# A graph layer on one core: node-block register loads merged, two carries a unit apart, gate values in PSUM, 32 column groups on VectorE

## The chip, the core and the metric

The kernel runs on one core of a Trainium2 chip. The core has five engines with queues of their own: TensorE (PE; its weight loads are PEld), VectorE (DVE), ScalarE (ACT), GpSimd (POOL) and SyncE (SP). The last two, and ScalarE, can start DMAs. An engine works through its queue in order; between engines semaphores wait and signal. The metric is the device time of one execution in microseconds, as the median of several runs.

## The reference

A message-passing layer over 12500 nodes with 128 features and 400000 edges, sorted by target node, followed by a GRU cell:

```python
h = relu(layernorm(x))                                     # 12500 x 128
m = relu(concat(h[src], h[dst], ea) @ w1 + b1) @ w2 + b2   # 400000 x 128, ea 400000 x 32
agg = segment_sum(m, dst, 12500)
gi, gh = agg @ w_ih + b_ih, h @ w_hh + b_hh                # split in r, z, n
r, z = sigmoid(gi_r + gh_r), sigmoid(gi_z + gh_z)
n = tanh(gi_n + r * gh_n)
out = x + (1 - z) * n + z * h
```

## The kernel before

**Layout.** A first stage normalizes all nodes, keeps h transposed in SBUF (`hT_all`, features on partitions, one column a node) and writes two products to DRAM, A = h @ w1[0:128] for the sources and B = h @ w1[128:256] + b1 for the targets. Then come the edges: 391 groups of 1024 edges, each handled as two *units* of 512, so 782 units. The Python loop over u writes every engine's instructions unit by unit; the order in which each engine works is fixed by it (the schedule is manual).

**A group.** TensorE forms the target's and the edge attributes' part of the message in `pre` (L763). The source's part comes in one of four ways, dealt out before the loop by the table `SPREAD`:

- GpSimd *gathers* rows of A by indirect DMA, 128 rows at a time, 8 gathers a group (L193). VectorE adds them to `pre` (L792, a saturating add that is also the relu). The first 9 groups gather rows of x.
- ScalarE *brings* a group's 1024 columns of `hT_all`, one 4-byte copy for each (L1103) into `HE_act`; the addresses come from register loads of 16. TensorE multiplies them by w1[0:128] into `pre` (L774), VectorE does the relu (L786). 29 groups.
- VectorE does the same for 31 groups, two columns an instruction (L1061), and reorders 256 columns at a time (L1073). Its register loads take up to 32 values (L1050).
- SyncE fetches single rows of A for 5 groups.

TensorE then sums the messages into windows of 32 nodes (L814).

**What sets the order.** ScalarE's and SyncE's groups are spread evenly over the units up to their use (`run_jobs`); VectorE's follow a table of what is due by each unit, and are fitted in small lots between its other work (`some`, `behind_long`, `in_time`). GpSimd's gathers are released by a credit, four times a unit, each tied behind the latest column instruction or VectorE instruction at that point (`let_go`). The register that a unit's steps set, `worked`, decides how many columns VectorE does behind the unit.

**The node blocks.** Every 14 groups a block of nodes is complete: 29 blocks, 26 of them 512 nodes wide. `node(b)` is a generator; one piece of it is written at the end of a unit, and `yield n` puts the next piece n units later. Its steps: the windows' sums are placed (L842, L847); what reaches over from the block before is added, in `carry` for the sums (`TOT`) and for the degrees (`DEG`) (L853, L856); the gates r, h_n, i_n and z follow (L892, L894, L896), in two PSUM banks by turns, "nd" and "misc"; ScalarE does the sigmoid of r (L902), tanh (L914) and the sigmoid of z (L916); VectorE the products and sums between (L906, L910, L920, L923, L926); TensorE transposes, VectorE adds x (L933), SyncE writes the output. Where a block begins is data, so its first node is a register value: `blk_i` holds the first nodes and `step_i` how far each block lies from the one before; VectorE (L861, L918), TensorE (L885) and SyncE (L830) each load theirs with `value_load`, which checks the value on the engine after the load. `last_node` is the same for the last block, in steps near the end of the loop.

Of the kernel before, what the change touches and what calls it, by code (L numbers as in the profile page):

```python
# [11 lines left out]
I32 = mybir.dt.int32  # L12
# [3 lines left out]
ET = mybir.EngineType  # L16
AF = mybir.ActivationFunctionType
ALU = mybir.AluOpType
# [36 lines left out]
STEP = {"act": 4, "sp": 4}  # L55
QUEUE = 10
ROW = 4 * D
SPREAD = {"dve": 31, "act": 29, "sp": 5}
START = {"dve": 14, "act": -6, "sp": 28}
SPARE = ("HE_act", "HE_dve", "G_sp")  # L60
NR = 12672
# [6 lines left out]
def tile_gnn(ctx: ExitStack, tc: tile.TileContext, x, src, srcT, dstT, dstP, eaT, eaP, w1, b1, w2T, b2,  # L68
# [253 lines left out]

    base_f = const.tile([1, NP], F32, name="base_f")
    blk_f = const.tile([1, NB], F32, name="blk_f")
    blk_i = const.tile([1, NB], I32, name="blk_i")
    off_f = const.tile([1, NB, 16], F32, name="off_f")
    off_i = const.tile([1, NB, 16], I32, name="off_i")
    base_i = const.tile([1, NB, 16], I32, name="base_i")
    step_f = const.tile([1, NB], F32, name="step_f")
    step_i = const.tile([1, NB], I32, name="step_i")  # L330
    step_c = const.tile([1, NB], F32, name="step_c")
    dloc = const.tile([128, T], F16, name="dloc")
    lim = const.tile([128, 2, NPL], F32, name="lim")
# [26 lines left out]
    def setup(pool):  # L360
        nc.vector.tensor_copy(base_f[:, 1:], base_d)
        nc.vector.memset(base_f[:, 0:1], 0.0)
        nc.vector.tensor_scalar(base_f, base_f, float(LAST), 0.0, op0=ALU.min, op1=ALU.max)
        yield
        nc.vector.tensor_copy(at_f[64:65, 512:512 + NP], base_f)
        nc.vector.tensor_tensor(at_f[64:65, :NP], at_f[64:65, 512:512 + NP], at_f[64:65, :NP], op=ALU.is_gt)
        nc.vector.tensor_reduce(beyond, at_f[64:65, :NP], AX.X, ALU.max)
        yield
        pm = ps1.tile([128, 512], F32, name="misc")
        nc.tensor.matmul(pm[:, :NP], ones, base_f, start=True, stop=True)  # L370
        nc.vector.tensor_copy(base_b[:, :, 0], pm[:, :NP])
        yield
        nc.vector.tensor_scalar(base_b[:, :, 1], pm[:, :NP], float(SHIFT), None, op0=ALU.add)
        for a in range(2):
            s = slice(V * a, V * (a + 1))
            nc.vector.tensor_scalar(node_of[s, :], base_b[s, :, a], place_c[s, :], float(-V * a),
                                    op0=ALU.add, op1=ALU.add)
        for b0, b1_, k0, n, w in groups:
            nc.vector.tensor_scalar(blk_f[:, b0:b1_], base_f[:, k0:k0 + (b1_ - b0 - 1) * n + 1:n], float(N - w),
                                    None, op0=ALU.min)  # L380
        yield
        nc.vector.tensor_copy(blk_i, blk_f)
        nc.vector.memset(off_f, 0.0)
        off_c = pool.tile([128, NB * 16], F32, name="off_c", bufs=1)[:1, :].rearrange("o (b n) -> o b n", n=16)
        yield
        nc.vector.memset(off_c, 0.0)
        nc.vector.tensor_tensor(step_f[:, 1:], blk_f[:, 1:], blk_f[:, :-1], op=ALU.subtract)
        nc.vector.memset(step_f[:, 0:1], float(BW))
        yield
        for b0, b1_, k0, n, w in groups:  # L390
            ks = base_f[:, k0:k0 + (b1_ - b0) * n].rearrange("o (b n) -> o b n", n=n)
            nc.vector.tensor_tensor(off_f[:, b0:b1_, :n], ks,
                                    blk_f[:, b0:b1_, None].to_broadcast([1, b1_ - b0, n]), op=ALU.subtract)
            nc.vector.tensor_scalar(base_i[:, b0:b1_, :n], ks, float(4 * D), None, op0=ALU.mult)
            nc.vector.tensor_scalar(off_c[:, b0:b1_, :n], off_f[:, b0:b1_, :n], float(w - V - SHIFT), 0.0,
                                    op0=ALU.min, op1=ALU.max)
        for b0, b1_ in [(0, 1), (1, NW + 1)] + [(b, b + 1) for b in range(NW + 1, NB)]:
            nc.vector.tensor_scalar(step_c[:, b0:b1_], step_f[:, b0:b1_], float(BLOCKS[max(b0 - 1, 0)][2]),
                                    float(LEAST[b0]), op0=ALU.min, op1=ALU.max)
        nc.vector.tensor_copy(off_i, off_c)  # L400
        yield
        nc.vector.tensor_tensor(off_f, off_f, off_c, op=ALU.not_equal)
        nc.vector.tensor_copy(step_i, step_c)
        nc.vector.tensor_tensor(step_f, step_f, step_c, op=ALU.not_equal)
        yield
        yield
        place(0)
# [417 lines left out]
        worked[0] = 1  # L825


    def block_start(b):
        k0, n, w = BLOCKS[b]
        g0 = nc.sync.value_load(blk_i[0:1, b:b + 1], min_val=0, max_val=N - w)  # L830
        xb = p3.tile([128, 4, D], F32, name="xb", bufs=2)[:w // 4, :, :]
        put(xb, x[bass.ds(g0, w), :].rearrange("(p i) f -> p i f", i=4))
        _, offs = nc.values_load_multi_w_load_instructions(
            off_i[0:1, b, 0:n], engines=[ET.PE], min_val=0, max_val=w - V - SHIFT,
            skip_runtime_bounds_check_because="clamped above")
        return g0, xb, offs
# [21 lines left out]
            nc.vector.memset(o[:, w:last], 0.0)  # L858

    def step_of(b):  # L860
        return nc.vector.value_load(step_i[0:1, b:b + 1], min_val=LEAST[b],  # L861
                                    max_val=BLOCKS[max(b - 1, 0)][2])

    def temp(w):
        return p3.tile([128, BW], F32, name="gt", bufs=3)[:, :w]
# [1 line left out]
    def node(b):  # L867
        w = BLOCKS[b][2]
        g0, xb, offs = block_start(b)
        pt = ps1.tile([128, 512], F32, name="nd")[:, :w]  # L870
        pd = ps1.tile([128, 512], F32, name="misc")[:, :w]
        nc.vector.tensor_copy(dcol[:, :len(offs) // 2], sums[:, :len(offs) // 2, D])
        zero(pt)
        for i in range(len(offs)):
            sum_of(b, pt, offs, i)
        zero(pd)
        for i in range(len(offs)):
            degree_of(b, pd, offs, i)
        d = step_of(b)
        yield 1  # L880
        carry(b, TOT, pt, d)
        carry(b, DEG[0:1, :], pd[0:1, :], d)
        worked[0] = 2
        yield 1
        g = nc.tensor.value_load(blk_i[0:1, b:b + 1], min_val=0, max_val=N - w)  # L885
        hT = hT_all[:, bass.ds(g, w)]

        def gate(name, i, with_h, with_s):
            c = slice(i * D, (i + 1) * D)
            ci = slice(2 * D, 3 * D) if i == 3 else c  # L890
            pg = ps1.tile([128, 512], F32, name=name)[:, :w]
            nc.tensor.matmul(pg, brow[:, c], DEG[:, :w], start=True, stop=False)  # L892
# [9 lines left out]
        nc.scalar.activation(r, pr, AF.Sigmoid)  # L902
        ph = gate("misc", 3, True, False)
        yield 1
        t = temp(w)
        nc.vector.tensor_tensor(t, r, ph, op=ALU.mult)  # L906
        pi = gate("nd", 2, False, True)
        worked[0] = 2
        yield 1
        nc.vector.tensor_tensor(t, t, pi, op=ALU.add)  # L910
        pz = gate("misc", 1, True, True)
        worked[0] = 2
        yield 2 if b < NW else 1
        nc.scalar.activation(t, t, AF.Tanh)  # L914
        z = temp(w)
        nc.scalar.activation(z, pz, AF.Sigmoid)  # L916
        yield 1
        gv = nc.vector.value_load(blk_i[0:1, b:b + 1], min_val=0, max_val=N - w)  # L918
# [7 lines left out]
        nc.vector.tensor_tensor(q, q, t, op=ALU.add)  # L926
# [12 lines left out]
        batch_store(b + FIRST)  # L939

    def last_node():
# [5 lines left out]
        zero(pd)  # L947
        for i in range(n):
            degree_of(b, pd, offs, i)
        d = step_of(b)  # L950
        g = nc.tensor.value_load(blk_i[0:1, b:b + 1], min_val=0, max_val=N - w)
        hT = hT_all[:, bass.ds(g, w)]
        gv = nc.vector.value_load(blk_i[0:1, b:b + 1], min_val=0, max_val=N - w)
        h = hT_all[:, bass.ds(gv, w)]
        pt = ps1.tile([128, 512], F32, name="nd")[:, :w]
        zero(pt)
# [500 lines left out]
```

## Time and profile before

| | |
|---|---|
| runs | 4668.68, 4675.16, 4681.94 us (median 4675.16) |
| the profiled execution | 4666.41 us, its span 4664.6 us |
| ScalarE busy | 3272.2 us (70%), 29939 instructions |
| VectorE busy | 2548.3 us (55%), 18124 instructions |
| TensorE busy | 2538.9 us (54%), 13193 matmuls |
| GpSimd busy | 2485.7 us (53%), 2614 instructions |
| DMA | 71 GB/s over the span |

A row of the groups reads: line, engine, operation, what it writes and reads, the shape, how often | busy microseconds, mean nanoseconds of one | idle microseconds of the engine just before, and what ended that idle time. A copy of four bytes is reported with 189 ns, but the next one starts before it has ended: busy time counts overlapping instructions once. A row of the waits reads: engine, tile and line that waited, who released it, microseconds in total, times, the longest. A row of the windows reads: from and to, length, then for PE, PEld, DVE, ACT and POOL the busy microseconds and the number of instructions, then TensorE's granted clock, the DMA share and GB/s. Operations marked "q" (register loads, checks) are the sequencer's and not counted as busy.

### The profile page before, as it was taken

How to read it: one execution, taken by the hardware profiler on the slowest of the kernel's cores; microseconds unless marked ns; L12 is line 12 of the kernel's file. 1: busy time of each engine (PE TensorE's matmuls, PEld its weight loads, DVE VectorE, ACT ScalarE, POOL GpSimd, SP SyncE). 2: the span in 40 equal slices, each digit the busy share in tenths (PEclk: the TensorE clock that was granted, in tenths of full speed). 3: DMA queues.
4: the chain of work that ended last, by engine and by line, in shares of the span. 5: the costliest groups of instructions: out<-in, count | busy, mean ns of one | idle time of the engine just before them, and what ended most of it. 6: DMA issues, size and time to landing. Idle time of an engine off the chain costs nothing. (4 is left out here: it accounts for less than half of the span.)

```text
span 4664.6 us, 96852 instructions
## 1 busy us (share of the span) xinstructions
PE 2538.9 (54%) x13193; PEld 1611.8 (35%) x13193; DVE 2548.3 (55%) x18124; ACT 3272.2 (70%) x29939; POOL 2485.7 (53%) x2614
## 2 busy tenths in 40 slices
PE   2465565565456455555555565455545454655657
PEld 2353342332234233323333333333323233323434
DVE  3475564564456446645654565456546555655655
ACT  2478667767767767777777767777776777676676
POOL 5345555555555555555555555555555555555551
PEclk7786767776667767776776667677767767767767
DMA  3322323222222223232222223232322322222221
GB/s 103 105 65 60 75 71 74 69 71 70 69 72 73 71 71 73 66 78 69 72 70 68 73 71 79 60 73 69 74 69 72 81 63 72 68 73 69 72 73 35
DMA packets 195490, 333.37 MB, mean 71 GB/s; under 512 B 68809, under 2 KB 117512, under 8 KB 194841
## 3 DMA queue, kind: packets, MB, share of 16 engines
q0 software_dynamic: 83360, 170.89, 16.0%
q1 hardware_dynamic: 111337, 156.20, 12.2%
q14 instruction: 539, 4.42, 0.3%
q8 instruction: 110, 1.80, 0.2%
q10 hardware_dynamic: 144, 0.07, 0.0%
HBM read 306.65 MB, written 20.24 MB: 70 GB/s over the span
## 5 line engine op out<-in xcount | busy, mean ns | idle before, releaser
L1103 ACT COPY HE_act<-hT_all 128x4 uint8 x29696 | 3169.2, 189 | 1255.9 <-issue 1223.5
L193 POOL DMA_INDIRECT G<-A,src_i x2512 | 2396.4, 954 | 2052.2 <-ACT HE_act L1103 1329.8
L1061 DVE SCALAR_TENSOR_TENSOR both<-hT_all 128x4 uint16 x15872 | 1365.4, 154 | 649.4 <-issue 635.6
L763 PE MATMUL pre<-RW,L 128*128 128x256 f32 x3128 | 1163.5, 499 | 536.3 <-DVE L L650 295.9
L763 PEld LDWEIGHTS pre<-RW,L 128*128 128x128 f32 x3128 | 681.9, 243 | 842.2 <-issue 433.3
L814 PE MATMUL seg<-RB,OH 128*32 128x129 f32 x6250 | 607.9, 325 | 270.2 <-DVE RB L792 158.4
L814 PEld LDWEIGHTS seg<-RB,OH 128*32 128x32 f32 x6250 | 334.4, 125 | 573.1 <-issue 308.9
L892 PE MATMUL nd<-DEG,brow 34*128 34x512 f32 (+2 forms) x112 | 89.0, 886 | 761.3 <-ACT gt L902 614.2
L792 DVE CUSTOM_DVE_ANT_0 RB<-pre,G 128x1024 f32<-128x1024 f32 x315 | 383.2, 1217 | 117.5 <-issue 62.9
L906 DVE TENSOR_TENSOR gt<-gt,misc 128x512 f32<-128x512 f32 (+2 forms) x28 | 18.9, 675 | 677.8 <-ACT gt L902 545.9
L892 PEld LDWEIGHTS nd<-DEG,brow 34*128 34x128 f32 x112 | 22.4, 248 | 775.7 <-ACT gt L902 620.8
L650 DVE TENSOR_TENSOR L<-L,seg 64x1024 f32<-64x1024 int32 x191 | 230.5, 1207 | 40.4 <-issue 16.4
L774 PE MATMUL pre<-w1a,HE_act 128*128 128x128 f32 x464 | 96.0, 328 | 255.0 <-ACT HE_act L1103 230.7
L786 DVE TENSOR_SCALAR RB<-pre 128x1024 f32<-128x1024 f32 x69 | 84.2, 1221 | 213.1 <-PE pre L774 154.4
L774 PEld LDWEIGHTS pre<-w1a,HE_act 128*128 128x128 f32 x464 | 90.0, 235 | 271.2 <-ACT HE_act L1103 235.6
L703 DVE TENSOR_TENSOR OH<-dloc,seg 128x512 f32<-128x512 f16 (+1 forms) x198 | 132.9, 672 | 17.6 <-issue 17.6
L842 PE MATMUL nd<-spot,sums 128*128 128x40 f32 x782 | 139.0, 358 | 2.8 <-DVE sums L823 2.8
L842 PEld LDWEIGHTS nd<-spot,sums 128*128 128x128 f32 x782 | 134.6, 270 | 13.7 <-issue 10.6
L1073 DVE COPY HE_dve<-both 128x1024 uint8<-128x1024 uint8 x124 | 88.6, 715 | 24.8 <-issue 15.7
L774 PEld LDWEIGHTS pre<-w1a,HE_dve 128*128 128x128 f32 x496 | 90.3, 226 | 14.1 <-remote 2.0
L920 DVE TENSOR_TENSOR gt<-hT_all,gt 128x512 f32<-128x512 f32 (+2 forms) x28 | 19.1, 680 | 134.3 <-ACT gt L914 109.3
L774 PE MATMUL pre<-w1a,HE_dve 128*128 128x128 f32 x496 | 89.3, 309 | 3.0 <-remote 1.7
(185 smaller groups left out, 1473.5 us busy)
## 6 DMA issues: line engine op xcount, KB each, us to landing
G_sp<-A SPq DMA_DIRECT2D x5120, 0.5 KB
L<-in_dstP SPq DMA_DIRECT2D x195, 256.0 KB
L<-in_eaP SPq DMA_DIRECT2D x195, 256.0 KB
G<-A,src_i POOLq DMA_INDIRECT x2512
RW<-B SPq DMA_DIRECT2D x782, 16.0 KB
xb<-in_x SPq DMA_DIRECT2D x26, 256.0 KB
out<-xb SPq DMA_DIRECT2D x26, 256.0 KB
xs<-in_x SPq DMA_DIRECT2D x11, 512.0 KB
```

The source lines that it names most:

```text
L193: fetched = nc.gpsimd.indirect_dma_start(out=G[k][:, j, a, :], out_offset=None, in_=x if k < RAW else A, in_offset=bass.IndirectOffsetOnAx ...
L650: recent[0] = nc.vector.tensor_tensor(o.rearrange("v (k e) -> v k e", k=m), i.rearrange("v (k e) -> v k e", k=m), SEGB[(k // 2) % 2][:2 * ...
L703: recent[0] = nc.vector.tensor_tensor(p, dloc[:, e0:e1, None].to_broadcast(shape), row[:, None, :].to_broadcast(shape), op=ALU.is_equal).ins
L763: nc.tensor.matmul(p[:, 2 * i:2 * i + 2, :], Ls[k // QP][:, c0:c0 + 128], RW[k % 4], start=True, stop=not raw)
L774: nc.tensor.matmul(p[:, 2 * i + a, :], cols, w1a, start=False, stop=n + 1 == len(l) or l[n + 1][1] != j)
L792: made = nc.vector._custom_dve(TENSOR_ADD_SAT, out=o, in0=p, in1=G[k].rearrange("p j a f -> p (j a) f")[:, c, :], s0=float("inf"), s1=0.0)
L814: nc.tensor.matmul(p[r0:r0 + V, :D + 1], OH[k][:, a * GRP + j, :], RB[k % 2][:, 2 * j + a, :D + 1], start=False, stop=all(b != a for _, _, ...
L842: nc.tensor.matmul(p[:, bass.ds(offs[i], V + SHIFT)], sums[:, slot(b, i), :D], spot[:, i % 2, :], start=False, stop=i == len(offs) - 1)
L892: nc.tensor.matmul(pg, brow[:, c], DEG[:, :w], start=True, stop=False)
L1061: recent[0] = nc.vector.scalar_tensor_tensor(self.both[:, e % PIECE // 2, :], column(second), 256.0, column(first), op0=ALU.mult, op1=ALU. ...
L1073: recent[0] = nc.vector.tensor_copy(hand[k].bitcast(U8)[:, p0 * 4:(p0 + PIECE) * 4].rearrange("p (n c b) -> p n c b", c=2, b=4), both.bitc ...
L1103: copied[0] = nc.scalar.copy(he[:, e * 4:e * 4 + 4], column(v)).ins
```

## The change

Four edits. VectorE's share in `SPREAD` goes from 31 groups to 32, so GpSimd gathers for one group less; the places of the other hand-brought groups shift by a group or so. In the node blocks the distance and the first node stand side by side in `off_i`; VectorE loads both in one load at the start of the block, and all engines load without the check on the engine. The two carries are written a unit apart in 26 blocks, which puts all later steps of these blocks a unit later. The value that goes into tanh and its result stay in the PSUM bank "nd" instead of an SBUF tile, and the z gate stays in "misc".

```diff
-SPREAD = {"dve": 31, "act": 29, "sp": 5}
+SPREAD = {"dve": 32, "act": 29, "sp": 5}
...
-        nc.vector.tensor_copy(step_i, step_c)
+        nc.vector.tensor_copy(off_i[:, :, 14], step_c)
+        nc.vector.tensor_copy(off_i[:, :, 15], blk_f)
...
+    def first_of(engine, b):
+        _, (g,) = nc.values_load_multi_w_load_instructions(
+            off_i[0:1, b, 15:16], engines=[engine], min_val=0, max_val=N - BLOCKS[b][2],
+            skip_runtime_bounds_check_because="clamped above")
+        return g
...
     def block_start(b):
         k0, n, w = BLOCKS[b]
-        g0 = nc.sync.value_load(blk_i[0:1, b:b + 1], min_val=0, max_val=N - w)
+        g0 = first_of(ET.SP, b)
...
     def step_of(b):
-        return nc.vector.value_load(step_i[0:1, b:b + 1], min_val=LEAST[b],
-                                    max_val=BLOCKS[max(b - 1, 0)][2])
+        _, (d, g) = nc.values_load_multi_w_load_instructions(
+            off_i[0:1, b, 14:16], engines=[ET.DVE], min_val=0, max_val=N - BLOCKS[b][2],
+            skip_runtime_bounds_check_because="clamped above")
+        return nc.s_assert_within(d, LEAST[b], BLOCKS[max(b - 1, 0)][2],
+                                  skip_runtime_bounds_check_because="clamped above"), g
...
-        d = step_of(b)
+        d, gv = step_of(b)
         yield 1
         carry(b, TOT, pt, d)
+        worked[0] = 2
+        if b < NW:
+            yield 1
         carry(b, DEG[0:1, :], pd[0:1, :], d)
         worked[0] = 2
         yield 1
-        g = nc.tensor.value_load(blk_i[0:1, b:b + 1], min_val=0, max_val=N - w)
+        g = first_of(ET.PE, b)
...
-        t = temp(w)
-        nc.vector.tensor_tensor(t, r, ph, op=ALU.mult)
-        pi = gate("nd", 2, False, True)
+        nc.vector.tensor_tensor(r, r, ph, op=ALU.mult)
+        t = gate("nd", 2, False, True)
         worked[0] = 2
         yield 1
-        nc.vector.tensor_tensor(t, t, pi, op=ALU.add)
+        nc.vector.tensor_tensor(t, r, t, op=ALU.add)
         pz = gate("misc", 1, True, True)
...
         nc.scalar.activation(t, t, AF.Tanh)
-        z = temp(w)
-        nc.scalar.activation(z, pz, AF.Sigmoid)
+        z = pz
+        nc.scalar.activation(z, z, AF.Sigmoid)
         yield 1
-        gv = nc.vector.value_load(blk_i[0:1, b:b + 1], min_val=0, max_val=N - w)
         q = r
```

In `last_node` the same loads are replaced: `step_of` and `first_of` in place of three `value_load`.

VectorE's queue at the two carries of a block in the middle of the program, before (`TOT` and `DEG` are the carried sums and degrees, `both` and `at` belong to the columns):

```order
L1061 SCALAR_TENSOR_TENSOR both<-hT_all 128x4 x3
L853 ISA
L853 TENSOR_TENSOR TOT<-nd,TOT 128x192
L856 COPY TOT<-nd 128x320
L853 ISA
L853 TENSOR_TENSOR DEG<-misc,DEG 1x192
L856 COPY DEG<-misc 1x320
```

and in the changed kernel, whose line numbers differ by a few (L790 is the addition of a gathered group):

```order
L857 TENSOR_TENSOR TOT<-nd,TOT 128x192
L860 COPY TOT<-nd 128x320
L1068 SCALAR_TENSOR_TENSOR both<-hT_all 128x4 x9
L1057 TENSOR_LOAD at
L1068 SCALAR_TENSOR_TENSOR both<-hT_all 128x4 x3
L790 ISA RB_179<-pre,G 128x8x128
L1068 SCALAR_TENSOR_TENSOR both<-hT_all 128x4 x9
L1057 TENSOR_LOAD at
L1068 SCALAR_TENSOR_TENSOR both<-hT_all 128x4 x7
L857 ISA
L857 TENSOR_TENSOR DEG<-misc,DEG 1x192
L860 COPY DEG<-misc 1x320
```

Two lots of columns with their register loads and a group's addition now stand between the carries.

VectorE's queue in the last block, before, from the last pair of windows' sums to the carry of the degrees:

```order
L861 TENSOR_LOAD step_i
L861 ISA x2
L953 TENSOR_LOAD blk_i
L953 ISA x2
L792 ISA RB_180<-pre,G 128x8x128
```

and in the changed kernel:

```order
L821 COPY sums<-seg_80 128x129
L865 TENSOR_LOAD off_i
L790 ISA RB_180<-pre,G 128x8x128
L857 ISA
L857 TENSOR_TENSOR DEG<-misc,DEG 1x192
```

One load without checks has taken the place of two loads with two checking steps each, ahead of a group's addition.

More of the change, by code (lines that the diff above doesn't have):

```diff
@@ L324, in tile_gnn @@
     blk_f = const.tile([1, NB], F32, name="blk_f")
-    blk_i = const.tile([1, NB], I32, name="blk_i")
     off_f = const.tile([1, NB, 16], F32, name="off_f")
@@ L381, in setup @@
         yield
-        nc.vector.tensor_copy(blk_i, blk_f)
         nc.vector.memset(off_f, 0.0)
@@ L949, in last_node @@
             degree_of(b, pd, offs, i)
-        d = step_of(b)
-        g = nc.tensor.value_load(blk_i[0:1, b:b + 1], min_val=0, max_val=N - w)
+        d, gv = step_of(b)
+        g = first_of(ET.PE, b)
         hT = hT_all[:, bass.ds(g, w)]
-        gv = nc.vector.value_load(blk_i[0:1, b:b + 1], min_val=0, max_val=N - w)
         h = hT_all[:, bass.ds(gv, w)]
```

1 line of the change is left out of this document (removed).

## The prediction

> **What bounds the kernel now.** I read the page's costliest groups first, to see which engine never rests, then the waits, to see who waits for whom.
>
> ```profile
> L1103 ACT COPY HE_act<-hT_all 128x4 uint8 x29696 | 3169.2, 189 | 1255.9 <-issue 1223.5
> L193 POOL DMA_INDIRECT G<-A,src_i x2512 | 2396.4, 954 | 2052.2 <-ACT HE_act L1103 1329.8
> L1061 DVE SCALAR_TENSOR_TENSOR both<-hT_all 128x4 uint16 x15872 | 1365.4, 154 | 649.4 <-issue 635.6
> L193 POOL DMA_INDIRECT G<-in_x,src_i x69 | 65.2, 945 | 21.9 <-issue 20.7 <-DMA src_i<-in_srcT 1.2
> ```
> ```profile
> POOL G L193 <- ACT HE_act L1103: 1329.8, 660, 16.0
> DVE gt L906 <- ACT gt L902: 545.9, 22, 36.2
> PE nd L892 <- ACT gt L902: 614.2, 22, 40.7
> ```
>
> Everyone waits for ScalarE. GpSimd holds its gathers for ScalarE's column copies (1329.8 us), and once in each node block VectorE and TensorE stand still until ScalarE has reached the sigmoid of r (545.9/22 = 24.8 us each time for VectorE). ScalarE itself waits for no engine between its first and its last copy: its idle time before the copies is 1255.9 us, of which 1223.5 are "issue", time in which it waited for nothing that the profile shows. Its timeline gives the two ends:
>
> ```profile
> 168.15 2.90 ACT L1103 COPY HE_act<-hT_all 128x4 uint8 x27 [1.07 <-DVE bn L255]
> ...
> 4629.23 3.58 ACT L1103 COPY HE_act<-hT_all 128x4 uint8 x36
> 4654.88 0.44 ACT L991 ACTIVATE gt<-pre 128x320 f32<-128x320 f32 x1 [22.07 <-PE pre L972]
> ```
>
> So the time is a head of 168.2 us, ScalarE's stretch of 4464.7 us up to 4632.8, and a tail of 31.8 us. The chain of waits on the page follows only the last microseconds and says nothing about this. An edit counts if it changes ScalarE's copies, its activations, its "issue" time, the head or the tail. What is that "issue" time? Four stretches of the windows view tell (per engine: busy us and instructions):
>
> ```profile
> 172.00:222.00 50.00, 5.73 (x24) 5.07 (x24) 9.86 (x45) 7.94 (x41) 37.81 (x41) 0.56 0.32 85
> 4430.00:4445.00 15.00, 0.00 (x0) 0.00 (x0) 0.00 (x0) 11.62 (x110) 8.38 (x10) 0.50 0.33 79
> 4574.00:4616.00 42.00, 32.00 (x171) 19.70 (x171) 30.66 (x210) 41.01 (x415) 0.00 (x0) 0.72 0.16 48
> ```
> ```profile
> 1271.12:1439.27 168.15, 94.76 (x500) 60.69 (x499) 95.65 (x689) 112.23 (x1028) 93.59 (x97) 0.72 0.30 73
> 1439.27:1577.33 138.06, 76.93 (x405) 47.50 (x405) 76.04 (x573) 107.72 (x1027) 76.25 (x81) 0.72 0.29 71
> ```
>
> From 4574 on there are no gathers: ScalarE does 415 instructions in 42.00 us (0.101 us each), busy for 41.01, although VectorE and TensorE work at full rate. From 4430 on they are silent and GpSimd sends 10 gathers in 15 us: ScalarE manages 110, worth 11.1 us, and loses 3.9. From 172 on 41 gathers follow each other closely and ScalarE does 41 instructions in 50 us. So gathers stop ScalarE. The last two rows are two of its groups, each of 1024 copies; the first is spread over 30 units of the program, the second over 24. The first takes 30.1 us longer for the same copies, and what it has more of is 16 gathers, 116 VectorE instructions and 95 matmuls. **The bound is ScalarE's copies plus what gathers, perhaps together with VectorE's and TensorE's work, take from them.**
>
> **The change part by part.**
>
> *The 32nd group.* It leaves GpSimd's list: 8 gathers fewer. What one takes from ScalarE is at least 3.9/10 = 0.39 us (the quiet stretch) and at most 30.1/16 = 1.88 us (all of the difference between the two groups). I take the middle, 1.1: 8 x 1.1 = **-8.8 us** (-3.1 to -15.0).
>
> VectorE gets 512 two-column instructions, four reorderings and 35 register loads more. On VectorE itself that is 512 x (1365.4 + 649.4)/15872 = 65 us, 2.3 us in each of 28 blocks, and the wait of 24.8 us hides it; with that cover gone it would be 65 us. What it takes from ScalarE no row isolates. Below, the stretch without gathers says nothing. Above, if all 1223.5 us of "issue" belonged to the 15872 column instructions, 0.077 us each. Two windows with nearly the same gathers give the same upper end:
>
> ```profile
> 1200.00:1600.00 400.00, 204.49 (x1063) 126.90 (x1063) 205.81 (x1511) 292.60 (x2721) 225.48 (x235) 0.71 0.28 69
> 2400.00:2800.00 400.00, 234.45 (x1161) 144.78 (x1159) 229.94 (x1685) 279.42 (x2587) 221.75 (x234) 0.68 0.29 71
> ```
>
> In the second ScalarE does 134 fewer (13.6 us) beside 174 more on VectorE and 98 more on TensorE: 0.078 if VectorE alone were to blame, 0 if TensorE were. I take 0.02, nearer to the stretch without gathers, the only row where the columns' effect stands alone: 512 x 0.02 = **+10.2 us** (0 to +39.4). That the register loads hold up VectorE is in the 649.4.
>
> Here the Trainium skill speaks against the change. Its page Perfetto Trace Analysis, section Optimizing Scalar/DVE Operations, says that GpSimd and VectorE share a read port of SBUF, so that moving work between those two might not help. The trace shows no such lengthening: a gather's instruction takes 954 ns beside the columns and 945 ns before there are any (the rows of L193). By that difference all 2512 would have lost 23 us in an engine that idles for 2052.
>
> *Register loads in one, unchecked.* The lines' own view gives what goes on VectorE and TensorE:
>
> ```profile
> L861 DVEq TENSOR_LOAD <-step_i x29: 304/307/619, 387.6 to 4638.2; - x29
> L861 DVEq FUSED_REGOPS  x29: 183/190/210, 388.0 to 4638.9; - x29
> L861 DVEq SEQ_ASSERT  x29: 23/23/41, 388.3 to 4639.1; - x29
> L918 DVEq TENSOR_LOAD <-blk_i x28: 304/308/535, 451.5 to 4627.2; - x28
> ```
> ```profile
> L885 PEldq TENSOR_LOAD <-blk_i x28: 300/306/320, 393.9 to 4605.4; - x28
> L885 PEldq FUSED_REGOPS  x28: 151/151/165, 394.3 to 4605.9; - x28
> ```
>
> VectorE saves 0.19 + 0.02 of checks, twice, and one load of 0.31: 0.73 us a block, 20 us in all; TensorE saves 0.17 a block. Both lie under the wait for the sigmoid and cost the end nothing; SyncE's same load only fetches the rows of x that the block adds in its last step. Some 260 small sequencer steps go from VectorE, TensorE and SyncE together. If such a step weighs on ScalarE like a column, that is -5.2, and 0 by the stretch without gathers; I take **-2.5 us**.
>
> *Carries a unit apart.* Nothing is added: the same four instructions, with columns and a group's addition between them. All later steps of 26 blocks come one unit (4464.7/782 = 5.7 us) later, ScalarE's three activations too. TensorE's gate r now waits for the later carry, behind whose wait VectorE holds columns and a group's addition; both reach it a good 20 us ahead of ScalarE, by the 24.8 us above, so this costs 0; if that lead were gone, up to 5.7 us a block.
>
> *Gates in PSUM.* The groups view, by line:
>
> ```profile
> L902 ACT ACTIVATE gt<-nd 128x512 f32<-128x512 f32 (+2 forms) x28 | 16.1, 576 | 0.0
> L914 ACT ACTIVATE gt<-gt 128x512 f32<-128x512 f32 (+2 forms) x28 | 17.2, 615 | 0.0
> L916 ACT ACTIVATE gt<-misc 128x512 f32<-128x512 f32 (+2 forms) x28 | 15.8, 565 | 0.6 <-issue 0.6
> L910 DVE TENSOR_TENSOR gt<-gt,nd 128x512 f32<-128x512 f32 (+2 forms) x28 | 18.6, 663 | 0.0
> L926 DVE TENSOR_TENSOR gt<-gt 128x512 f32<-128x512 f32 (+2 forms) x28 | 18.8, 670 | 0.7 <-issue 0.6
> ```
>
> These are ScalarE's own instructions, on the path. Reading PSUM (L902) is 39 ns shorter than reading SBUF (L914). The tanh changes at both its ends, the sigmoid of z at its output: at most 3 x 39 ns x 28 = -3.3 us. Writing to PSUM no row shows; it could cost as much as reading saves, +3.3. I take **-2 us**. On VectorE an operand in PSUM (L910) costs the same as two in SBUF (L926), and the wait hides more. The banks are held longer, but the next user of "nd" (the transpose) needs the result anyway, and "misc" next serves the next block.
>
> The same section of the Trainium skill gives an access overhead of about 93 ns on SBUF and 51 on PSUM for ScalarE, and 60 and 125 for VectorE. As an estimate by that page ScalarE would save 3 x 42 ns x 28 = 3.5 us and the sum would be 1.5 us lower. For VectorE the two rows above show no such 65 ns.
>
> *Tail.* In the last block VectorE's addition stood behind two checked loads:
>
> ```profile
> 4638.22 0.29 DVE L823 COPY sums<-seg 128x129 f32<-128x129 f32 x1
> 4640.03 1.23 DVE L792 CUSTOM_DVE_ANT_0 RB<-pre,G 128x1024 f32<-128x1024 f32 x1 [1.52 <-PE pre L763]
> ```
>
> The second load and both checks go, 0.31 + 2 x 0.21 = 0.7 us of the idle 1.52; TensorE's product is then late next. **-0.5 us** (0 to -0.7).
>
> Sum: -8.8 + 10.2 - 2.5 - 2 - 0.5 = **-3.6 us**. Against the profiled execution (4666.41 us, span 4664.6) that is 4662.8; this execution lies 8.75 us below the median of the runs, 4675.16, so I predict **4671.5 us**.
>
> **The rivals.**
>
> *Gathers set the pace (faster).* If the whole 30.1 us is the gathers', one costs 1.88 us and a column nothing: -15.0 - 3.3 - 0.7 = -19.0 us, **4656**. For it: the stretch without gathers, where columns cost nothing. Against it: the quiet stretch, where a gather cost 0.39.
>
> *Columns weigh on ScalarE while gathers run (slower).* At the upper price the 512 instructions cost +39.4; with the rest of the sum (-13.8) that is +25.6 us, **4701**. For it: the two windows of 400 us. Against it: those windows also differ in matmuls. It turns slower than 0.3% (14 us) from (14 + 13.8)/512 = 0.054 us a column on.
>
> *Nothing reaches the path.* The credit that GpSimd's gathers are dealt by spreads the remaining ones evenly over the same copies, ScalarE loses as much to them as before, PSUM makes no difference: **4675**.
>
> **How the numbers follow.** The forecast has 0.47, the faster rival 0.25, the slower one 0.14, no effect 0.14. A measurement of this kernel can tell about 0.3%, 14 us, from no change. So faster 0.25, within 0.3% 0.61, slower 0.14. For the range, the lower end takes the faster rival and 4 us of scatter (4652). The upper end is the forecast with a column at 0.05 and no gain but the gathers': -8.8 + 25.6 = +16.8, 4692. The slower rival stays outside with its 0.14.
>
> **What would show it.** Right: L193 down by 8, L1061 at 16384, ScalarE's "issue" time within 15 us of 1223.5, its two PSUM activations some 30 to 80 ns shorter, the wait for the sigmoid down by 1 to 3 us a block, and the tail near 31 us. The faster rival: "issue" down by about 15. The slower one: "issue" up by some 30 at the same number of copies. The forecast is wrong in kind if ScalarE's activations or copies show a wait for VectorE or TensorE, or the wait at the sigmoid is gone: then a PSUM bank or the later carry has become the bound.

## The result and the profile after

The changed kernel takes 4694.18 us (median of 20 runs, 4678.18 to 4705.78), the kernel before 4675.59 us (20 runs, 4667.81 to 4683.70): a ratio of 1.0036 [1.0028, 1.0045], slower by 18.6 us. The prediction was 4671.5 us, with no measurable change as the likeliest case. The profiled execution took 4692.93 us with a span of 4690.7, against 4666.41 and 4664.6 before.

The experiments ran on five other chips, on which the kernel before takes 3322 to 3328 us. ScalarE's "issue" time ahead of its copies, 1223.5 us in the trace of before, is 28 to 38 us in the traces of the experiments. So their differences are read against the kernel before on the same chip. One of the six runs of e1 took 6052 us, in a slow state, and its ratio leaves that run out.

First the page's costliest groups of the changed kernel (columns as before: busy and mean | idle just before and what ended it).

```profile
L1110 ACT COPY HE_act<-hT_all 128x4 uint8 x29696 | 3169.9, 189 | 1280.5 <-issue 1246.4
L193 POOL DMA_INDIRECT G<-A,src_i x2504 | 2385.5, 953 | 2081.8 <-ACT HE_act L1110 1393.0
L1068 DVE SCALAR_TENSOR_TENSOR both<-hT_all 128x4 uint16 x16384 | 1407.3, 154 | 685.0 <-issue 672.6
```

ScalarE makes the same 29696 copies with the same busy time (3169.2 before), and stands idle before them for 24.6 us more (1255.9 before); 22.9 of that are "issue". GpSimd has lost 8 gathers, VectorE has gained 512 column instructions. The waits of the changed kernel (waiting engine, tile and line, releaser, us in total, times, longest) show that VectorE still stands at the sigmoid of r:

```profile
ACT HE_act L1110 <- issue: 1246.4, 2120, 1.9
...
ACT gt L912 <- issue: 1.9, 2, 1.0
...
DVE gt L915 <- ACT gt L912: 548.3, 23, 34.3
```

That is 548.3/23 = 23.8 us each time, one us less than before. No row has ScalarE wait for VectorE or TensorE in a block between its first and its last copy. Its timeline has the two ends of its stretch:

```profile
4655.76 3.58 ACT L1110 COPY HE_act<-hT_all 128x4 uint8 x36
...
4680.58 0.44 ACT L998 ACTIVATE gt<-pre 128x320 f32<-128x320 f32 x1 [21.24 <-PE pre L979]
```

The last copy ends at 4659.34 (4632.81 before), and 31.4 us remain to the end of the span (31.8 before). So all of the 26.1 us by which the two profiled spans differ came in ScalarE's stretch of copies, as "issue", beside the same work. About 8 of the 26 are scatter: the profiled execution of before lies 9.2 us below its median, that of the changed kernel 1.3 us below.

### The profile page after: what moved, and what is told of

The parts are those of the page before. It is cut to its first block, busy times and chain, and to the rows that moved or that the text cites. A ratio compares the mean times of both kernels' runs of the same rounds, so it can differ in the third digit from the quotient of the medians.

```text
span 4690.7 us, 97156 instructions
## 1 busy us (share of the span) xinstructions
PE 2562.7 (55%) x13209; PEld 1620.9 (35%) x13209; DVE 2591.3 (55%) x18640; ACT 3272.6 (70%) x29939; POOL 2474.9 (53%) x2606
## 5 line engine op out<-in xcount | busy, mean ns | idle before, releaser
L1110 ACT COPY HE_act<-hT_all 128x4 uint8 x29696 | 3169.9, 189 | 1280.5 <-issue 1246.4
L193 POOL DMA_INDIRECT G<-A,src_i x2504 | 2385.5, 953 | 2081.8 <-ACT HE_act L1110 1393.0
L1068 DVE SCALAR_TENSOR_TENSOR both<-hT_all 128x4 uint16 x16384 | 1407.3, 154 | 685.0 <-issue 672.6
L812 PE MATMUL seg<-RB,OH 128*32 128x129 f32 x6250 | 623.7, 331 | 413.6 <-DVE RB L790 218.2
L790 DVE CUSTOM_DVE_ANT_0 RB<-pre,G 128x1024 f32<-128x1024 f32 x314 | 382.0, 1217 | 122.1 <-issue 65.9
L915 DVE TENSOR_TENSOR gt<-gt,misc 128x512 f32<-128x512 f32 (+2 forms) x28 | 18.9, 675 | 650.5 <-ACT gt L912 548.3
L846 PE MATMUL nd<-spot,sums 128*128 128x40 f32 x782 | 129.1, 341 | 5.7 <-DVE sums L821 4.3
L846 PEld LDWEIGHTS nd<-spot,sums 128*128 128x128 f32 x782 | 124.9, 253 | 16.5 <-issue 12.0
L542 PE MATMUL pre<-w1a,hT_all 128*128 128x128 f32 x196 | 52.1, 419 | 68.8 <-issue 30.4
```

Of the source, the lines that this page charges most:

```text
L193: fetched = nc.gpsimd.indirect_dma_start(out=G[k][:, j, a, :], out_offset=None, in_=x if k < RAW else A, in_offset=bass.IndirectOffsetOnAx ...
L790: made = nc.vector._custom_dve(TENSOR_ADD_SAT, out=o, in0=p, in1=G[k].rearrange("p j a f -> p (j a) f")[:, c, :], s0=float("inf"), s1=0.0)
L812: nc.tensor.matmul(p[r0:r0 + V, :D + 1], OH[k][:, a * GRP + j, :], RB[k % 2][:, 2 * j + a, :D + 1], start=False, stop=all(b != a for _, _, ...
L846: nc.tensor.matmul(p[:, bass.ds(offs[i], V + SHIFT)], sums[:, slot(b, i), :D], spot[:, i % 2, :], start=False, stop=i == len(offs) - 1)
L1068: recent[0] = nc.vector.scalar_tensor_tensor(self.both[:, e % PIECE // 2, :], column(second), 256.0, column(first), op0=ALU.mult, op1=ALU. ...
L1110: copied[0] = nc.scalar.copy(he[:, e * 4:e * 4 + 4], column(v)).ins
```

## The experiments

Ratios, with their 95% intervals, are to the kernel before on the same chip; they are formed from the single runs and so are not exactly the quotients of the two medians beside them.

| | edit | us | before, us | ratio |
|---|---|---|---|---|
| e1 | before, VectorE 32 groups | 3384.88 | 3325.38 | 1.0185 [1.0172, 1.0198] |
| e6 | the same again | 3384.38 | 3324.70 | 1.0188 [1.0174, 1.0202] |
| e2 | after, VectorE 31 groups | 3318.16 | 3325.38 | 0.9980 [0.9971, 0.9988] |
| e7 | the same again | 3318.57 | 3324.70 | 0.9980 [0.9971, 0.9989] |
| e5 | after | 3367.19 | 3324.70 | 1.0121 [1.0105, 1.0136] |
| e18 | after again | 3368.79 | 3321.99 | 1.0132 [1.0117, 1.0148] |
| e8 | before, VectorE 30 groups | 3339.09 | 3327.97 | 1.0036 [1.0022, 1.0050] |
| e9 | after without later carry and PSUM | 3367.88 | 3327.97 | 1.0118 [1.0103, 1.0134] |
| e3 | before without the source part of 8 groups (64 gathers) | 3298.33 | 3325.38 | 0.9926 [0.9913, 0.9939] |
| e4 | before, 1984 columns repeated in place | 4661.22 | 3325.38 | 1.4028 [1.4010, 1.4046] |
| e10 | before, 512 more columns | 3324.02 | 3327.97 | 0.9993 [0.9984, 1.0002] |
| e15 | the same again | 3321.22 | 3321.99 | 0.9999 [0.9990, 1.0008] |
| e11 | before, 35 loads done twice | 3365.57 | 3327.97 | 1.0114 [1.0097, 1.0131] |
| e16 | the same again | 3366.48 | 3321.99 | 1.0130 [1.0114, 1.0145] |
| e14 | before, both additions | 3383.22 | 3321.85 | 1.0185 [1.0171, 1.0199] |
| e17 | the same again | 3385.13 | 3321.99 | 1.0189 [1.0175, 1.0203] |
| e12 | after, all loads of 32 values | 3349.95 | 3321.85 | 1.0084 [1.0071, 1.0098] |
| e13 | e12 with 31 groups | 3319.62 | 3321.85 | 0.9994 [0.9985, 1.0003] |

### The change taken apart (e1, e2)

e1 is the kernel before with one number changed, e2 the changed kernel with that number put back.

```diff
-SPREAD = {"dve": 31, "act": 29, "sp": 5}
+SPREAD = {"dve": 32, "act": 29, "sp": 5}
```

> The kernel before with the 32nd group on VectorE and nothing else of the change. Column theory (512 more column instructions with their register loads take some 0.05 us each from ScalarE while gathers run, 8 gathers fewer give 3 to 9 us back): +15 to +25 us against before, ScalarE's issue time up by about as much. Block theory (the later carry, the loads or the PSUM banks slow the kernel): within 5 us of before.

> The changed kernel with 31 groups on VectorE, so only the three edits in the node blocks. Column theory: -5 to 0 us against before. Block theory: +15 to +20 us.

The 32nd group alone costs 59.5 us, and the three edits to the node blocks gain 7.2: on this chip the loss is the group's. That version, the three edits with 31 groups, is faster than both kernels on these chips. The loads of VectorE for columns in e1 and in e2 (duration in ns: shortest, median, longest), and e2's row of columns:

```profile
L1050 DVEq TENSOR_LOAD <-at x1291: 591/1680/3201, 176.0 to 3326.7; - x185
```
```profile
L1057 DVEq TENSOR_LOAD <-at x1214: 593/2098/3344, 178.1 to 3260.6; - x174
L1068 DVE SCALAR_TENSOR_TENSOR both<-hT_all 128x4 uint16 x15872 | 1351.2, 156 | 498.3 <-issue 490.2
```

The kernel before has 1237 of these loads. So the group brings 54, and not the 35 that the prediction gave it: 35 is the whole change's number, after the edits to the node blocks have taken away 19. The page and ScalarE's waits of e1:

```profile
L1103 ACT COPY HE_act<-hT_all 128x4 uint8 x29696 | 2993.3, 189 | 69.7 <-issue 32.4
```
```profile
ACT gt L902 <- PE nd L896: 90.4, 15, 17.4
ACT gt L914 <- DVE gt L910: 61.0, 22, 7.9
```

Here ScalarE's "issue" is 32.4 us, and it waits in the node blocks: at the sigmoid of r for TensorE's gate, which stands behind VectorE's carry, and at tanh for VectorE's sum. In the trace of before it was VectorE that waited at that sigmoid. ScalarE's copies are busy for 2993 of e1's 3383 us, and what lengthens the rest here is its waiting for VectorE's work.

### The price of a gather, and a first doubling of the columns (e3, e4)

```diff
+    for i in range(8):
+        k = 40 + 40 * i
+        while k in mode:
+            k += 1
+        mode[k] = "none"
...
-        if u in HE or k in hand:
+        if u in HE or k in hand or mode.get(k) == "none":
```

> The kernel before without the source part in 8 of the gathered groups: 64 gathers fewer, nothing put in their place. It prices a gather: at 0.39 us (quiet stretch) -25 us, at 1.1 us -70 us, at 1.88 us (whole difference of the two copy groups) -120 us. If VectorE's and TensorE's work alone took ScalarE's time, 0.

27.05 us less for 64 gathers: 0.42 us each, near the 0.39 that the prediction took from the quiet stretch as its lower end. The 8 gathers that the change drops are worth 3.4 us at this price, not 8.8. It is a price of this chip, where ScalarE shows no such "issue" time.

```diff
+                if e % 16 == 0:
+                    recent[0] = nc.vector.scalar_tensor_tensor(
+                        self.both[:, e % PIECE // 2, :], column(second), 256.0, column(first),
+                        op0=ALU.mult, op1=ALU.add).ins
```

> The kernel before with every eighth column instruction of VectorE done twice, 1984 more, without more register loads, matmuls or fewer gathers. Column theory with the price in the instruction itself: 0.05 us each, +100 us. If the price is in the register loads or in the places of the groups: within 15 us of before.

1336 us more, 0.67 us for each of 1984 repeats. The repeat writes the place that the instruction just ahead of it wrote. Groups, then waits, of e4:

```profile
L1061 DVE SCALAR_TENSOR_TENSOR both<-hT_all 128x4 uint16 x15872 | 1516.1, 157 | 1406.1 <-issue 1404.1
L1065 DVE SCALAR_TENSOR_TENSOR both<-hT_all 128x4 uint16 x1984 | 324.0, 163 | 69.6 <-DVE both L1061 1.4
```
```profile
ACT gt L902 <- PE nd L896: 982.8, 28, 47.2
```

The repeats' own row (L1065) has 324.0 + 69.6 us, 0.20 us each. More lies ahead of the other columns, which stand in "issue" for 1404.1 us against 490.2 in e2 on the same chip. Summed over the trace, VectorE is idle for 1526 us inside its register loads, 528 in e2: 4.9 of its instructions start during a load, 8.6 in e2. So less work stands queued ahead of a load when there are repeats. That a repeat holds the queue until the instruction ahead of it has written would explain this; no run shows it. ScalarE waits at every one of the 28 sigmoids. It shows that ScalarE follows VectorE when VectorE is late, but the price of a column isn't in it, since the repeats changed what the loads cost. It was done anew as e10.

### The same three on another chip (e5, e6, e7)

> The changed kernel itself, beside before on the same chip. If the issue time of ScalarE (some 1220 us in the profile before) is there, 4.68 to 4.70 ms against 4.675; if the chip shows none of it, as in the four runs ahead, 3325 us for before and about 3325 + 59 - 7 = 3377 us here: the 32nd group costs, the rest of the change saves a little.

> The kernel before with the 32nd group on VectorE alone. Column theory: slower than the changed kernel by 0 to 10 us in either condition, since the other edits save a little. Block theory: equal to before.

> The changed kernel with 31 groups on VectorE. Column theory: 0 to 10 us faster than before in either condition. Block theory: as slow as the changed kernel.

The changed kernel, e1's and e2's, as they were: +42.5, +59.7 and -6.1 us. ScalarE's waits in the blocks, of e5 first and of e7 second:

```profile
ACT nd L923 <- DVE nd L919: 74.3, 18, 8.2
ACT gt L912 <- PE nd L906: 55.1, 12, 13.4
```
```profile
ACT nd L923 <- DVE nd L919: 39.0, 14, 6.5
ACT gt L912 <- PE nd L906: 35.3, 8, 16.1
```

129.4 against 74.3 us: 55.1 more for the 32nd group, where the medians differ by 48.6 and the two profiled executions by 56.1. The group's cost is paid in these two waits.

### Fewer groups, and the node-block edits singly (e8, e9)

e8 sets the number to 30. e9 is the changed kernel with the carries together and tanh and sigmoid of z in SBUF again; its edits to the loads remain:

```diff
-        worked[0] = 2
-        if b < NW:
-            yield 1
...
+        t = temp(w)
...
-        z = pz
-        nc.scalar.activation(z, z, AF.Sigmoid)
+        z = temp(w)
+        nc.scalar.activation(z, pz, AF.Sigmoid)
```

> The kernel before with 30 groups on VectorE instead of 31, 8 gathers more. Theory that VectorE is full (its own time is what ends the units, 65 us for a group): -20 to -50 us, until gathers and ScalarE hold the units instead. Theory that columns cost ScalarE a little each while gathers run: about -10 us. If the 31st to 32nd step is a matter of the places of the groups alone: within 5 us.

> The changed kernel without the later carry and with gate values in SBUF: the 32nd group and the unchecked loads in one. Full-VectorE theory: the loads give VectorE back 20 us, so 15 to 20 us faster than the 32nd group alone (3384), 3365 to 3370, as the whole change. If the later carry or PSUM is what helped: 3380 to 3385.

With 30 groups it is 11.1 us slower, and not faster as a full VectorE alone would have it. VectorE's waits in e8 have a row that is new:

```profile
DVE RB L792 <- DMA G<-A,src_i: 112.9, 35, 7.6
```

VectorE now waits for gathered rows, for 112.9 us where the versions with 31 groups (e2, e7, e10, e15) have 8.0 at most. So with 30 groups gathers come late, and with 32 VectorE's own work does: 31 is better than both neighbours.

e9 is 39.9 us above before; e1, the group alone, is 59.5 and 59.7 above, the changed kernel 42.5 and 46.8. e9 has the same 1291 loads for columns as e1. So the unchecked, merged loads by themselves give back 20 us of the group's cost, and all three node-block edits 13 to 17: the gain at 32 groups is the loads', and the later carry and PSUM together bring nothing here, if they don't cost a few microseconds.

### Loads or columns (e10, e11, e14)

Two kinds of work that the 32nd group brings, each added alone to the kernel before; the 35 loads are the prediction's number, not the group's 54. e10 writes 512 extra column instructions into a tile that nothing reads, one after each 31st, so without the stall of e4. e11 does every 35th register load twice, the second straight behind the first, which makes 35 more.

```diff
+                if self.done % 31 == 0:
+                    i = self.done // 31
+                    if i % 64 == 0:
+                        self.more = pj.tile([128, 64, 4], U16, name="more")
+                    recent[0] = nc.vector.scalar_tensor_tensor(
+                        self.more[:, i % 64, :], column(second), 256.0, column(first),
+                        op0=ALU.mult, op1=ALU.add).ins
```
```diff
-            self.vals, self.e = list(vals), self.e + n
+            vals = list(vals)
+            self.loads = getattr(self, "loads", 0) + 1
+            if self.loads % 35 == 0:
+                _, again = nc.values_load_multi_w_load_instructions(
+                    at[r:r + 1, self.e:self.e + n], engines=[ET.DVE], min_val=H_AT,
...
+                vals[1::2] = list(again)[1::2]
+            self.vals, self.e = vals, self.e + n
```

> The kernel before with 512 column instructions more, spread evenly, written to a tile that nobody reads; no register load, no matmul and no gather changes. By VectorE's row (86 ns busy each) that is 44 us of its time. Full-VectorE theory: +30 to +45 us. Column theory at 0.05 us: +25 us. If a group's cost lies in its register loads: under +10 us.

> The kernel before with every 35th of VectorE's register loads for columns done twice: 35 loads more, half of the values taken from the second; no column more. By the idle time before the columns (649 us over 1237 loads, 0.5 us each) that is 18 us. Full-VectorE theory: +15 to +40 us, the more the less of a load is hidden. Column theory: 0.

> The kernel before with both the 512 column instructions and the 35 loads: the 32nd group's work on VectorE without its matmuls, its places and the 8 gathers. If the two together fill VectorE where each alone found room: +50 to +65 us, as the 32nd group alone (+60). If the loads alone count: +38. The rest of the 60 would then lie in where the groups stand.

The columns cost nothing (-4.0 us, its interval reaches 1.0002), the loads 37.6 us, both together 61.4: as much as the whole group in e1 and e6. So both draw on the same room on VectorE: the columns, free by themselves, weigh once the loads have used it up. That the group's own cost divides in this way is not shown, for the loads added here are placed otherwise than the group's (e16 below).

### All four on one chip (e15 to e18)

Those three stood on two chips, so they stand here side by side, with the changed kernel beside them.

> The kernel before with 512 more two-column instructions, into a tile that nothing reads. On a chip where the kernel before takes some 3325 us: within 6 us of it by either theory, as before. Where it takes some 4675 us with over 1000 us of issue at ScalarE's copies: the theory that loads make the 32nd group dear says within 10 us; the theory that columns weigh on ScalarE while gathers run says 20 to 30 us more, in ScalarE's issue time.

> The kernel before with 35 column loads done twice. Where the kernel before takes some 3325 us: +38 us as before (30 to 46). Where it takes some 4675 us: by the theory of the loads 20 us or more, by the theory of the columns under 10.

> Both additions in one kernel. Where the kernel before takes some 3325 us: +60 us (55 to 65), which is more than the sum of the two alone on the same chip if the room on VectorE is what they share; if they simply add, +38. Where it takes some 4675 us: about 30 us by either theory.

> The changed kernel beside them on one chip. Where the kernel before takes some 3325 us: +42 us. Where it takes some 4675 us: +18 us, and the two kernels with one addition each then show which of them it is.

On this chip, too, the kernel before takes the shorter of its two times, 3322 us. The columns alone come to -0.8 us, the loads to +44.5, both to +63.1, 19 more than the sum of the two; the changed kernel is at +46.8. ScalarE's waits of e15, e16 and e17, in this order:

```profile
ACT gt L902 <- PE nd L896: 45.4, 11, 9.8
ACT gt L914 <- DVE gt L910: 44.7, 16, 7.3
```
```profile
ACT gt L902 <- PE nd L896: 71.0, 16, 11.8
ACT gt L914 <- DVE gt L910: 54.1, 18, 5.5
```
```profile
ACT gt L902 <- PE nd L896: 84.4, 17, 12.5
ACT gt L914 <- DVE gt L910: 67.8, 20, 6.1
```

90.1, 125.1 and 152.2 us: beside e15, 35.0 and 62.1 more, of the 51.8 and 69.7 by which the profiled executions differ. And VectorE's column instructions in the groups view, e15 first and e16 second:

```profile
L1061 DVE SCALAR_TENSOR_TENSOR both<-hT_all 128x4 uint16 x15872 | 1377.8, 154 | 500.8 <-issue 489.9
```
```profile
L1068 DVE SCALAR_TENSOR_TENSOR both<-hT_all 128x4 uint16 x15872 | 1348.1, 154 | 569.4 <-issue 558.1
```

The 35 extra loads don't show as busy time (this row is even lower than e15's). They appear as 68.2 us more of "issue" ahead of the columns. The loads' own rows are in the source view, of e16 (duration in ns: shortest, median, longest):

```profile
L1050 DVEq TENSOR_LOAD <-at x1237: 595/2096/3356, 176.7 to 3312.0; - x177
```
```profile
L1056 DVEq TENSOR_LOAD <-at x35: 1097/1680/2206, 255.2 to 3280.3; - x35
```

The 35 loads sum to 62.9 us, of which 44.5 reach the end. VectorE is idle for 62.3 of the 62.9: it starts next to nothing while a doubled load runs. Inside the 1237 ordinary loads of the same trace it is idle for 543.1 of 2173.0 us, 0.44 us each, because work queued ahead of the load (8.5 instructions on average) still runs. So VectorE gets no further instruction while a load lasts, as these 35 show; the queue covers three quarters of an ordinary one, and nothing of one that stands straight behind another.

That is where e11 and e16 differ from the group. From e2 to e1 (77 loads more, and without the node-block edits) VectorE's idle time inside these loads grows by 46.4 us (527.6 to 574.0) and its busy time by 55.4 (2516.2 to 2571.6). In the group both can weigh, and how its 60 us divide between them stays open.

### Longer loads (e12, e13)

The price lies in the loads, so fewer and longer ones were tried: 32 values whenever there is room for a load, 1024 loads in place of 1272 for the same columns.

```diff
-MOST, SOME, FEW = 32, 24, 16
+MOST, SOME, FEW = 32, 32, 32
```

> The changed kernel with all of VectorE's column loads of 32 values (1024 instead of 1272, the same 32768 values). If the price of a load is its time in the sequencer, about 0.1 us for a load and 0.064 for a value by the rows (1.1 us for 16, 2.1 for 32): -20 us against the changed kernel, 3345. If what counts is the part of a load that the queued columns don't cover, longer loads leave more uncovered: 0 to +30 us, up to 3395.

> The same with 31 groups on VectorE (992 loads instead of 1214). Time-in-the-sequencer theory: 0 to -15 us against 3318, so faster than both kernels. Uncovered-part theory: 0 to +20 us.

At 32 groups, 28.1 us above before; the changed kernel is 42.5 and 46.8 above, so longer loads take back a third or more. At 31 groups, 2.2 us below before, which can't be told from none, and a little worse than e7's -6.1. VectorE's waits in e12:

```profile
DVE both L1068 <- issue: 664.6, 932, 2.2
```

More "issue" than the 513.0 of the changed kernel on e18's chip, at 248 fewer loads: a load of 32 stands longer than the queue covers, and VectorE is idle for 0.59 us inside each, 0.44 in e18. The sum of the loads is 24.7 us less, 2213.5 against 2238.2, near the 20 that the expectation's first theory counts on; but by the "issue" time VectorE should have lost. So why it is faster at 32 groups isn't settled; the best version run stays e2 and e7.

## Why the prediction was wrong

**The 32nd group's term failed.** It had two halves. The first was what a column takes from ScalarE: "I take 0.02, nearer to the stretch without gathers", +10.2 us. On the recorded chip ScalarE's "issue" went up by 22.9 us at the same copies, which is the sign that the slower rival was given ("issue" up by some 30). No run took the change apart on this chip, so the term is had by subtraction: what closes the measured sum is 18.6 + 3.4 for the gathers at e3's price + 2.4 for PSUM + 0.6 for the tail (both below) = 25.0 us, 0.049 us a column instruction, and 0.038 to 0.054 over the interval of the ratio (13 to 21 us). That is inside the bounds of 0 to 0.077 and near the 0.054 at which the rival turns the result; the value taken was too low. The rival's time and its sign came nearer than the forecast's; its mechanism, columns that weigh on ScalarE while gathers run, is not shown by that. The row that I went by, the stretch from 4574 us on, is right for itself: without gathers columns take nothing. But the columns of the change run beside gathers, where that row says nothing, and the two windows with the same gathers, which did speak of that place, served only for the upper bound. Whether the 25 us are the columns' or the loads' could not be tried in that condition. The changed kernel's trace has the loads' count and length:

```profile
L1057 DVEq TENSOR_LOAD <-at x1272: 596/1704/3128, 313.4 to 4629.9; - x182
```

Before there were 1237 of them. Summed over all of them in the two traces they take 2167.7 us before and 2235.3 us after, 67.6 more, and VectorE is idle inside them for 572.1 and 617.9 us, 45.8 more. That this delays ScalarE on the recorded chip is not shown: ScalarE waits for no engine there.

**The second half was the cover.** "On VectorE itself that is ... 65 us ... and the wait of 24.8 us hides it; with that cover gone it would be 65 us." On the recorded chip the cover held: the column instructions' busy and idle time together grew by (1407.3 + 685.0) - (1365.4 + 649.4) = 77.5 us, and 23.8 us are left at each sigmoid. On the other chips it was gone, since ScalarE reaches the sigmoid there before VectorE has the carry done, and e1 and e6 paid 59.5 and 59.7 us. There a column instruction with the idle time ahead of it takes (1351.2 + 498.3)/15872 = 0.117 us (e2), 60 us for 512, so this way of pricing the work held. "That the register loads hold up VectorE is in the 649.4" is true of loads on average; where a load stands is what the average hides, and e11 and e16 paid 1.1 and 1.3 us for each of 35 that nothing covered.

**The gathers' term was too large by the one price measured.** It was -8.8 at 1.1 us each; e3 measured 0.42 us, where ScalarE shows next to no "issue" time. What one takes on the recorded chip was not measured; at the prediction's own 1.1 the term left for the columns would be 30.4 us, 0.059 each. The -2.5 for 260 sequencer steps wasn't measured there either, and is left out of both; with it they are 2.5 us larger. The count was right (2504 in L193). "So gathers stop ScalarE" does not hold on every chip: the last section has the same 41 gathers in 50 us beside 486 instructions of ScalarE.

**The faster rival and "nothing reaches the path"** both fall with the sign of the result.

**PSUM was right.** The groups by line of the changed kernel:

```profile
L912 ACT ACTIVATE gt<-nd 128x512 f32<-128x512 f32 (+2 forms) x28 | 16.2, 578 | 1.9 <-issue 1.9
L923 ACT ACTIVATE nd<-nd 128x512 f32<-128x512 f32 (+2 forms) x28 | 15.8, 565 | 0.0
L925 ACT ACTIVATE misc<-misc 128x512 f32<-128x512 f32 (+2 forms) x28 | 14.8, 528 | 0.2 <-issue 0.2
L919 DVE TENSOR_TENSOR nd<-gt,nd 128x512 f32<-128x512 f32 (+2 forms) x28 | 18.9, 674 | 0.5 <-issue 0.5
```

tanh went from 615 to 565 ns and the sigmoid of z from 565 to 528: 28 x 87 ns = 2.4 us, against the 2 forecast. VectorE's write into PSUM takes 674 ns against 663 into SBUF, and it is covered on the recorded chip.

**Loads, carries, tail.** The two-value load is 0.53 us, where the sum had it at the 0.31 of a single one; two loads and their checks were 1.04 us before, so VectorE saves 0.51 us a block and not 0.73:

```profile
L865 DVEq TENSOR_LOAD <-off_i x29: 529/534/942, 387.3 to 4664.0; - x29
```

"Cost the end nothing" fits the recorded chip as far as its waits show, and is wrong on the others, where VectorE is late: there the loads' edit makes the 13 to 17 us by which the changed kernel is below e1 and e6. The later carry cost nothing in either: no wait of ScalarE in a block on the recorded chip, and e9 within 3 to 7 us of the changed kernel on the others. The tail's -0.5 was -0.64. In the timeline of VectorE's last block the addition stands 0.88 us behind TensorE, 1.52 before:

```profile
4663.94 0.29 DVE L821 COPY sums<-seg 128x129 f32<-128x129 f32 x1
4665.11 1.22 DVE L790 CUSTOM_DVE_ANT_0 RB<-pre,G 128x1024 f32<-128x1024 f32 x1 [0.88 <-PE pre L761]
```

**What stays open.** On the recorded chip, which of the four edits lengthens ScalarE's "issue" time by 23 us, and by which route. That it is the 32nd group is inferred: on the other chips it alone costs time, though by a wait of ScalarE for VectorE's work that the recorded chip does not show.

## What to carry to other kernels

Before work is handed to an engine that looks 55% busy, add up its register loads, which the busy time leaves out: here 2168 us of them stand beside 2548 us of busy time. Then look at what is queued ahead of each: 35 more, straight behind other loads, cost 38 to 44 us where 512 more instructions, spread out, cost none. Price a moved piece of work by the stretches in which it will run, beside the same neighbours, and not by the stretch that isolates it best. Where an engine's idle time covers an edit, ask which engine's slowness makes that idle time; when it went, the same number that hid 65 us cost 60.

## What the runs showed of the hardware

The same program took 4675 us on one chip and 3322 to 3328 on five others. The instructions are not slower: a copy is 189 ns in both, a gather's instruction 953 ns on the one and 957 on e18's chip, a load of VectorE 2095 and 2096 ns in the median. What differs most is that ScalarE stands idle in "issue" before its copies; besides, its first copy begins at 168.3 us and not at 93.8. The page of e18, on a chip of the shorter kind, beside the recorded 1280.5 and 2081.8:

```profile
L1110 ACT COPY HE_act<-hT_all 128x4 uint8 x29696 | 2992.8, 189 | 68.2 <-issue 31.8
L193 POOL DMA_INDIRECT G<-A,src_i x2504 | 2395.2, 957 | 774.4 <-issue 581.7
```

On the recorded chip there are 2120 such idle pieces of 0.59 us on average (1246.4/2120), and in the prediction's windows they were the most where gathers stood closest. But gathers alone don't make them. The changed kernel at the first gathers, on the recorded chip and in e18, in the windows view:

```profile
172.00:222.00 50.00, 5.17 (x24) 4.52 (x24) 9.86 (x44) 7.64 (x40) 37.81 (x41) 0.54 0.32 85
```
```profile
94.60:144.60 50.00, 27.08 (x172) 21.92 (x173) 42.46 (x184) 48.55 (x486) 37.82 (x41) 0.81 0.43 108
```

The same 41 gathers stand beside 40 instructions of ScalarE on the one chip and 486 on the other, and TensorE and VectorE, too, do far less on the first. SyncE shows it as well: its register moves for the rows it fetches, in the source view (ns: shortest, median, longest), the recorded chip first and e18 second:

```profile
L110 SPq MOVE G_sp<-A x5120: 2/29/1447, 372.8 to 4547.4; - x197
```
```profile
L110 SPq MOVE G_sp<-A x5120: 29/29/73, 229.2 to 3252.8; - x197
```

So what stops ScalarE there is not ScalarE's alone. The granted TensorE clock is lower there, 0.71 in the changed kernel against 0.79 in e18, but a low clock by itself doesn't bring the pauses: e4, slow for another reason, had 0.698 and only 30.9 us of "issue" ahead of ScalarE's copies. What makes that chip differ no run shows.

The other finding is e4's: writing again the place just written cost 0.20 us an instruction in its own row, and with these repeats the register loads stood less covered, with 1.23 us of idle time in each where e2 has 0.43.
